# Group-norm sums taken over channels and halves of the positions on TensorE instead of over positions on VectorE

## The chip, the cores and the metric

The kernel runs on one core of one Trainium2 chip. The time is device microseconds of that core for one execution; the number that is compared is the median of several runs of the same program.

## What is computed

The input x has the shape (16, 256, 32, 32). Two layers run one after the other, each as a residual around a group norm:

```
x = x + layer0(gn(x))     # attention with 4 heads of 32, then a feed-forward part with gelu
x = x + layer1(gn(x))     # a gated state-space scan (Mamba) with 512 channels and 64 states
```

gn normalizes over 16 groups. It takes the tensor as (B, H, W, C) = (16, 256, 32, 32), so "H" is what the kernel calls its 256 channels, and a group is two neighbouring elements of the last axis:

```
g = v.reshape(B_, H_, W_, G, C_ // G)
m = mean(g, axis=(1, 2, 4));  s = var(g, axis=(1, 2, 4))
(g - m) / sqrt(s + 1e-5)
```

In the kernel an image is two tiles of 128 partitions (channels) by 1024 positions. A position p belongs to the group (p // 2) % 16. The mean of a group is thus a sum over all 256 channels and over 64 of the 1024 positions, divided by 16384. The two layers need one group norm each per image, 32 in all.

## The kernel before, in words

**The scan.** The long part is the scan of layer 1. An image is 256 units; in each, VectorE runs one scan instruction over 128 rows by 1024 positions (L928). A unit needs: a load of 512 KB from DRAM (dub, L906, seven buffers, issued six units ahead), a product on GpSimd (L911, four units ahead), a pair of bf16 matmuls into a PSUM tile of two banks (decay, L920), and the exponential of it on ScalarE (L922). There are two such PSUM tiles (pool aps), so the matmuls for unit n+2 wait until the scan of unit n has freed its tile. After each eight units the states are multiplied with C on TensorE (outputs, L953: 32 small matmuls per unit; L959 copies on ScalarE; in the first unit of the next eight, 64 small matmuls more, L965). Once per image, at units 7 and 8, ScalarE spreads C out into the tile cd that these matmuls read (spread_c, L937).

**The side stream.** While image b is scanned, everything else for image b+1 runs beside it: first_norm (the first group norm, L351 on), the gate and store of image b-1, attention_layer, and scan_inputs, which begins with the second group norm. These are Python generators. Each yield ends a step and gives its share, a length in units. The main loop turns the shares into a schedule: rate_for finds one rate so that all shares of an image fill 247 units, gap gives a step of share 1 exactly one unit, a longer one share/rate units, a shorter one its share. In each unit the order written is: load, product, outputs, scan, decay, and then the step of the side stream that is due. Each of TensorE, ScalarE, VectorE and GpSimd executes in the order in which the program was written (the last lines of the kernel chain them by hand), and the DMAs are all issued by SyncE in order.

**PSUM.** Beside the scan, psum(name) hands out one of two single banks (pool mm). Before the scan begins, the whole of image 0 is prepared with nothing beside it, and free_bank gives, in turn, a bank of mm and the two halves of a double bank of aps; a half not yet used waits in the list spare.

**The group norm** (group_norm, L259 to L297) has these steps, with their shares: sum of the first tile (1); sum of the second and the mean (1); subtract and square, once per tile (1 and 1); sum of the first square tile (1); sum of the second and the variance (1); Ln and Exp on ScalarE (2.2); multiply, once per tile (0.6 and 0.6). A sum is one reduce on VectorE over a whole tile with 16 results per partition (sum_of, L262). The sums over channels are two matmuls of the matrix avg (all 1/256) with these 16 columns (mean_of, L267). L279 scales the mean in PSUM. L281 subtracts it, L283 squares, L296 multiplies. `along` issues one DMA after each step from a list: in the first norm the loads of the position embedding and of the gate of image b-1, in the second the store of xs, the loads of rel (read by L617) and of the weights.

**Neighbours that the prediction uses.** layer_norm takes its means with pairs of 128x512 fp32 matmuls (L304) straight on the values. scan_inputs goes on after its norm with the additions of rel (L617) and the projections z (L640, two 128x512 matmuls per step). gate_and_store begins with L836 on VectorE and L840 on GpSimd.

Of the kernel before, what the change touches and what calls it, by code (L numbers as in the profile page):

```python
# [11 lines left out]
F32 = mybir.dt.float32  # L12
BF16 = mybir.dt.bfloat16
AF = mybir.ActivationFunctionType
ALU = mybir.AluOpType
AX = mybir.AxisListType
# [3 lines left out]
P = 128  # L20
C = 256
KC = C // P
L = 1024
HL = 512
NG = 16
# [25 lines left out]
def attention_then_scan_kernel(  # L51
# [18 lines left out]
    nc = tc.nc  # L70
    B = x.shape[0]

    def pool(name, bufs, **kw):
        return ctx.enter_context(tc.tile_pool(name=name, bufs=bufs, **kw))

    const = pool("const", 1)
# [4 lines left out]
    small = pool("small", 2)  # L81
# [12 lines left out]
    alone, spare = cycle((mm, aps)), []  # L94

    def bank(src, name):
        return src.tile([P, HL], F32, name=name, tag="mm" if src is mm else "av")

    def free_bank(name):
        if spare:  # L100
            return spare.pop()
        if next(alone) is mm:
            return bank(mm, name)
        both = aps.tile([P, L], F32, name=name, tag="a")
        spare.append(both[:, hs(1)])
        return both[:, hs(0)]

    def psum(name, dims=P):
        return (bank(mm, name) if beside["scan"] else free_bank(name))[:dims]
# [7 lines left out]
    def work(name, n=L):  # L117
        return wide.tile([P, L + 2 + CONV], F32, name=name, tag="wide")[:, :n]
# [4 lines left out]
    def hs(h):  # L123
        return ts(h, HL)
# [16 lines left out]
    make_identity(nc, ident)  # L141
    avg = const.tile([P, P], F32, name="avg")
    nc.vector.memset(avg, 1.0 / C)
    eps = const.tile([P, 1], F32, name="eps")
    nc.vector.memset(eps, 1e-5)

# [15 lines left out]
    for k in range(ND):  # L162
# [4 lines left out]
        for j in range(2):  # L167
# [3 lines left out]
                start=(j == 0), stop=(j == 1),  # L171
# [32 lines left out]
    t = work("ones_s")[:1]  # L204
# [3 lines left out]
    for k in range(KC):  # L208
        t = work("rel_s").rearrange("p (i j) -> p i j", j=32)
# [38 lines left out]
    def grouped(ap):  # L248
        return ap.rearrange("p (h g t) -> p h g t", g=NG, t=2)

    def over_group(s):
        return s.unsqueeze(1).unsqueeze(3).to_broadcast([P, L // (2 * NG), NG, 2])
# [4 lines left out]


    def group_norm(src, dst):  # L259
        def sum_of(part, s, k):  # L260
            view = part.rearrange("p (h g t) -> p g h t", g=NG, t=2)
            nc.vector.tensor_reduce(s[:, k, :], view, AX.XY, ALU.add)  # L262

        def mean_of(s, name):
            m = psum(f"{name}_ps")[:, :NG]
            for k in range(KC):
                nc.tensor.matmul(m, avg, s[:, k, :], start=(k == 0), stop=(k == KC - 1))  # L267
            return m

        per = C / (C * L / NG)  # L270
        s = small.tile([P, KC, NG], F32, name="gn_s", tag="gn_s")
        sum_of(src[0], s, 0)
        yield 1
        sum_of(src[1], s, 1)
        m = mean_of(s, "gn_m")
        yield 1
        s = small.tile([P, KC, NG], F32, name="gn_q", tag="gn_s")
        qs = []
        nc.vector.tensor_scalar(m, m, per, None, ALU.mult)  # L279
        for k in range(KC):  # L280
            nc.vector.tensor_tensor(grouped(dst[k]), grouped(src[k]), over_group(m), ALU.subtract)  # L281
            q = work("gn_sq")
            nc.scalar.activation(q, dst[k], AF.Square)  # L283
            qs.append(q)
            yield 1
        sum_of(qs[0], s, 0)
        yield 1
        sum_of(qs[1], s, 1)
        del qs, q
        v = mean_of(s, "gn_v")  # L290
        yield 1
        nc.scalar.activation(v, v, AF.Ln, bias=eps, scale=per)
        nc.scalar.activation(v, v, AF.Exp, scale=-0.5)
        yield 2.2
        for k in range(KC):
            nc.vector.tensor_tensor(grouped(dst[k]), grouped(dst[k]), over_group(v), ALU.mult)  # L296
            yield 0.6  # L297
# [53 lines left out]
    def first_norm(b, besides=()):  # L351
        xs, tok = [], []
        kept = state[b]["kept"] = dram.tile([C, L], F32, name="kept", tag="kept")
        if "x" in state[b]:
            xs = state[b].pop("x")
        else:
            for go in fetches(xs, x[b]):
                go()
            yield 0.4
        gn = [work("gn") for _ in range(KC)]  # L360
        yield from along(group_norm(xs, gn), fetches(tok, pos) + [None] * 3 + list(besides))
        for k in range(KC):
            nc.gpsimd.tensor_tensor(tok[k], tok[k], gn[k], ALU.add)
            nc.sync.dma_start(kept[ts(k, P), :], tok[k])
            yield 0.6
# [231 lines left out]
    def scan_inputs(b):  # L597
# [8 lines left out]
        for t in xp:  # L606
            nc.vector.memset(t[:, 0:1], 0.0)
            nc.vector.memset(t[:, L + 1 : L + 2], 0.0)
        rels = []
        yield from along(  # L610
            group_norm(xs, body),
            [partial(nc.sync.dma_start, st["xr"][ts(k, P), :], xs[k]) for k in range(KC)]
            + fetches(rels, rel) + bring,
# [274 lines left out]
    def load(n):  # L888
        b, k, q, e, i = units[n]
        st = state[b]  # L890
        if (k, q, e, i) == (0, 0, 0, 0):
            bt = hst.tile([P, L], F32, name="bt", tag="bt")
            ct = hst.tile([P, L], F32, name="ct", tag="ct")
            for v, lo in ((bt, 0), (ct, NS)):
                src = st["rows"][lo : lo + NS, :]
                nc.sync.dma_start(v, src.unsqueeze(1).to_broadcast([NS, 2, L]))
            blocks[b] = {"bt": bt, "ct": ct}
        if i == 0:
            pieces = blk.tile([P, HL], BF16, name="pieces", tag="pieces")
            rows = ds(((k * 4 + q) * 2 + e) * 48, 48)  # L900
            for hf in range(2):
                nc.sync.dma_start(pieces[ds(64 * hf, 48)], st["dps"][rows, hs(hf)])
            blocks[b, k, q, e] = pieces
        du = dutp.tile([P, L], F32, name="dub", tag="dub")
        src = st["dus"][ts(k, P)].rearrange("(q j i e) c -> q e i j c", q=4, j=2, i=SLOTS)[q, e, i]
        nc.sync.dma_start(du, src.unsqueeze(0).to_broadcast([NS, 2, L]))  # L906
        loaded[n] = du
# [87 lines left out]

    AHEAD, LEAD = 6, 4
    beside["scan"] = True
    for n in range(AHEAD):
        load(n)
    for n in range(LEAD):  # L1000
# [123 lines left out]
```

## Time and profile before

| | |
|---|---|
| median of 3 runs | 12974.16 us (12973.16 to 13009.8) |
| the profiled execution | 12999.14 us |
| its span, first to last instruction | 12997.4 us |
| first scan to last scan | 435.3 to 12948.1 us |
| VectorE busy | 11576.5 us (89%) |
| TensorE matmuls busy | 9794.6 us (75%) |
| ScalarE busy | 7531.4 us (58%) |
| GpSimd busy | 10007.5 us (77%) |
| mean granted TensorE clock | 0.799 |
| reduces of the norm (L262), 128 of them | 1.16 to 1.22 us each |

The profile is of one execution. A group in it stands for all instructions of one line and one kind, with the busy time, the mean duration, and the idle time of the engine just before them with what ended it. "PE" is the matmul part of TensorE and "PEld" its weight loads; one fp32 matmul appears as two records. The granted clock is a share of full speed. 435 us pass before the first scan; the following images take 785 to 801 us each from scan 0 to scan 0, and the last one, with little beside it, 608.

### The profile page before, as it was taken

What the parts mean: (1) busy time and instruction counts of PE and PEld (TensorE: products, weight loads), DVE (VectorE), ACT (ScalarE), POOL (GpSimd) and SP (SyncE); (2) the same over time, 40 slices, a digit from 0 to 9 for tenths busy, and PEclk for the clock granted to TensorE, in tenths of its full rate; (3) what the DMA queues carried; (4) which work ended last, traced back from release to release, by engine and by line L of the source; (5) the groups of instructions that cost most, each with busy time, mean ns of one, the idle gap of its engine ahead of it and who ended that gap; (6) DMA issues with size and microseconds to landing.
All of it is one profiled execution on the core that took longest, in us unless ns stands there. A gap on an engine that the chain in (4) does not pass through costs nothing.

```text
span 12997.4 us, 424123 instructions
## 1 busy us (share of the span) xinstructions
PE 9794.6 (75%) x186800; PEld 5486.9 (42%) x186800; DVE 11576.5 (89%) x7464; ACT 7531.4 (58%) x10421; POOL 10007.5 (77%) x4201
## 2 busy tenths in 40 slices
PE   6676877868778687786878768687786877868777
PEld 2344444444444444444444434444344444444445
DVE  3789999899999899898999999999998998989998
ACT  2465664656646566565665656656565664656654
POOL 0588877878778787787878878787787877878798
PEclk8887977878778797887879878797787978868755
DMA  1467666675666766667666666766667666676676
GB/s 51 166 218 245 206 215 224 221 243 203 212 224 220 241 204 214 230 217 239 207 228 224 217 231 211 241 210 215 225 220 241 209 215 224 224 239 202 224 252 229
DMA packets 1038400, 2820.09 MB, mean 217 GB/s; under 512 B 290370, under 2 KB 368451, under 8 KB 1036548
## 3 DMA queue, kind: packets, MB, share of 16 engines
q1 hardware_dynamic: 1036548, 2792.97, 63.2%
q8 instruction: 1459, 23.90, 0.7%
q14 instruction: 393, 3.22, 0.1%
HBM read 2513.82 MB, written 261.62 MB: 214 GB/s over the span
## 4 chain that ended last, share of the span: by engine, by line
DVE 37%; PE 29%; issue 13%; ACT 10%; DMA 7%; POOL 3%; SPq 1%; DVEq 0%; POOLq 0%; ACTq 0%
DVE h L928 26%; PE yb L953 5%; DVE mx L417 5%; ACT a L922 5%; PE a L920 4%; DMA dub<-dus 4%; PE av L492 3%; POOL dub L911 2%; PE st_ps L504 2%; PE z_ps L640 2%; PE g_ps L689 2%; PE yb L965 1%; PE m_ps L865 1%; DMA xs<-ud 1%; DVE u L675 1%
## 5 line engine op out<-in xcount | busy, mean ns | idle before, releaser
L911 POOL TENSOR_TENSOR dub<-dub,bt 128x1024 f32<-128x1024 f32 x4096 | 9781.6, 2410 | 2841.4 <-DMA dub<-dus 2555.3
L928 DVE TENSOR_TENSOR_SCAN h<-a,dub 128x1024 f32<-128x1024 f32 x4096 | 9217.0, 2280 | 798.1 <-ACT a L922 492.2
L922 ACT ACTIVATE a<-a,acol 128x1024 f32<-128x1024 f32 x4096 | 4463.0, 1090 | 3177.0 <-PE a L920 3112.4
L920 PE MATMUL a<-pieces,pick 48*128 48x512 bf16 x8192 | 1915.4, 458 | 2380.2 <-DVE h L928 2258.4
L953 PEld LDWEIGHTS yb<-h,cd 128*32 128x32 f32 x131072 | 2511.0, 129 | 2808.0 <-issue 1281.3
L953 PE MATMUL yb<-h,cd 128*32 128x64 f32 x131072 | 3283.5, 253 | 472.1 <-ACT y L959 331.8
L920 PEld LDWEIGHTS <-pick 48*128 48x128 bf16 x8192 | 606.0, 95 | 2779.1 <-issue 2368.6
L959 ACT COPY y<-yb 128x256 f32<-128x256 f32 x2048 | 763.0, 373 | 811.5 <-PE yb L953 803.5
L436 PE MATMUL s_ps<-k,q 32*64 32x512 f32 x4092 | 823.4, 617 | 93.4 <-DVE mx L417 93.4
L417 DVE TENSOR_REDUCE mx<-s_ps 128x1 f32<-128x512 f32 x1023 | 657.5, 698 | 20.0 <-PE s_ps L436 20.0
L492 PE MATMUL av<-pt,vv 128*64 128x512 f32 x2048 | 600.1, 666 | 2.8 <-ACT sums L481 1.6
L512 ACT ACTIVATE pt<-st_ps 128x512 f32<-128x512 f32 x1024 | 553.8, 597 | 71.0 <-PE st_ps L504 70.1
L965 PE MATMUL yb<-turn,y 128*32 128x16 f32 x32768 | 590.8, 214 | 4.3 <-issue 3.3
L504 PE MATMUL st_ps<-sp 33*128 33x512 f32 x2048 | 577.8, 640 | 3.3 <-ACT pt L512 3.3
L965 PEld LDWEIGHTS yb<-turn,y 128*32 128x32 f32 x32768 | 573.1, 159 | 5.1 <-issue 3.7
L969 ACT COPY yo<-yb 128x128 f32<-128x128 f32 x512 | 136.0, 266 | 627.0 <-PE yb L965 619.7
L689 PE MATMUL g_ps<-w,xp 128*128 128x256 f32 x1464 | 457.9, 452 | 0.0
L689 PEld LDWEIGHTS g_ps<-w,xp 128*128 128x128 f32 x1464 | 369.1, 326 | 67.1 <-issue 58.1
L436 PEld LDWEIGHTS s_ps<-k,q 32*64 32x64 f32 x4092 | 193.1, 130 | 435.2 <-DVE mx L417 417.0
L675 DVE SCALAR_TENSOR_TENSOR u<-up,cwh,u 128x1024 f32<-128x1024 f32 x192 | 305.1, 1589 | 27.9 <-ACT u L667 27.7
L865 PE MATMUL m_ps<-w,xs 128*128 128x256 f32 x1024 | 317.7, 460 | 11.8 <-POOL xs L840 11.8
L865 PEld LDWEIGHTS m_ps<-w,xs 128*128 128x128 f32 x1024 | 262.2, 328 | 57.6 <-issue 26.0
(177 smaller groups left out, 6805.3 us busy)
## 6 DMA issues: line engine op xcount, KB each, us to landing
dub<-dus SPq DMA_DIRECT2D x4096, 512.0 KB
dps<-pc SPq DMA_DIRECT2D x384, 128.0 KB
pieces<-dps SPq DMA_DIRECT2D x1024, 48.0 KB
xs<-in_x_dram SPq DMA_DIRECT2D x64, 512.0 KB
xs<-kept SPq DMA_DIRECT2D x64, 512.0 KB
zs<-z SPq DMA_DIRECT2D x64, 512.0 KB
ud<-u SPq DMA_DIRECT2D x64, 512.0 KB
dus<-du SPq DMA_DIRECT2D x64, 512.0 KB
```

Source lines behind the costliest of these rows:

```text
L417: nc.vector.tensor_reduce(mx[:, g, c, hf : hf + 1], s, AX.X, ALU.max)
L436: nc.tensor.matmul(waiting[g][0][ts(e, 64)], q4[r, ts(c, 64)], k4[r, hs(hf)], start=True, stop=True,)
L492: nc.tensor.matmul(av[ts(e, 2 * DH)], vv[j // (NJ // 2)][:, j % (NJ // 2), 2 * pair + e, :], pts[e], start=(j == 0), stop=(j == NJ - 1),)
L504: nc.tensor.matmul(s, ka[r, ts(j, P)], qa[r, hs(hf)], start=True, stop=True)
L689: nc.tensor.matmul(ps[:, ts(q, C)], xp[k][:, ds(first + t, P, 4)], wg_s[:, k, t, :], start=(k == 0 and t == 0), stop=False,)
L911: nc.gpsimd.tensor_tensor(v, v, blocks[units[n][0]]["bt"], ALU.mult)
L920: nc.tensor.matmul(a[:, hs(hf)], w, pieces[r], start=True, stop=True)
L922: nc.scalar.activation(a, a, AF.Exp, scale=acol[:, at : at + 1])
L928: nc.vector.tensor_tensor_scan(now["h", e][:, i, :], decays.pop(n), loaded.pop(n), 0.0, ALU.mult, ALU.add)
L953: nc.tensor.matmul(yb[ts(g, 32), ts(s, 64)], cd[:, at // 16, ts(c, 32)], hbuf[:, :, at : at + 8], start=(c == 0), stop=(c == 1),)
L959: nc.scalar.copy(y2[:, r], yb[:, :256])
L965: nc.tensor.matmul(some[ts(r, 32), x], y2[:, r, x:256:8], turn[:, x], start=True, stop=True)
```

## The change

The sums of the norm are no longer taken over positions first. sum_of now gives the values themselves, 512 columns at a time, to TensorE as the moving operand, against a new constant matrix share (all 1/16384): for each of the two tiles and each half of the positions, one 128x512 matmul, all four added up in one PSUM bank. This leaves 512 column sums, the same on all partitions. mean_of then reduces these 512 to 16 on VectorE (one reduce from PSUM into a small SBUF tile). For the mean, ScalarE copies the 16 numbers back into the first columns of the bank, where L281 reads them as before; the scaling L279 is gone, since share has the whole factor. For the variance, Ln reads the 16 numbers from SBUF and writes PSUM. The mean gets a step of its own (share 1), and the reduce for the variance moves into the step of Ln and Exp. The bank of each norm half is taken at the first sum instead of after the second. spare is emptied when the scan begins.

```
+    share = const.tile([P, P], F32, name="share")
+    nc.vector.memset(share, 1.0 / (C * L / NG))
...
     def group_norm(src, dst):
-        def sum_of(part, s, k):
-            view = part.rearrange("p (h g t) -> p g h t", g=NG, t=2)
-            nc.vector.tensor_reduce(s[:, k, :], view, AX.XY, ALU.add)
-
-        def mean_of(s, name):
-            m = psum(f"{name}_ps")[:, :NG]
-            for k in range(KC):
-                nc.tensor.matmul(m, avg, s[:, k, :], start=(k == 0), stop=(k == KC - 1))
+        def sum_of(part, sums, k):
+            for h in range(2):
+                nc.tensor.matmul(
+                    sums, share, part[:, hs(h)],
+                    start=(k == 0 and h == 0), stop=(k == KC - 1 and h == 1),
+                )
+
+        def mean_of(sums):
+            m = small.tile([P, NG], F32, name="gn_s", tag="gn_s")
+            nc.vector.tensor_reduce(
+                m, sums.rearrange("p (h g t) -> p g h t", g=NG, t=2), AX.XY, ALU.add
+            )
             return m

-        per = C / (C * L / NG)
-        s = small.tile([P, KC, NG], F32, name="gn_s", tag="gn_s")
+        s = psum("gn_m_ps")
         sum_of(src[0], s, 0)
         yield 1
         sum_of(src[1], s, 1)
-        m = mean_of(s, "gn_m")
-        yield 1
-        s = small.tile([P, KC, NG], F32, name="gn_q", tag="gn_s")
+        yield 1
+        m = s[:, :NG]
+        nc.scalar.copy(m, mean_of(s))
+        yield 1
         qs = []
-        nc.vector.tensor_scalar(m, m, per, None, ALU.mult)
         for k in range(KC):
             nc.vector.tensor_tensor(grouped(dst[k]), grouped(src[k]), over_group(m), ALU.subtract)
             q = work("gn_sq")
             nc.scalar.activation(q, dst[k], AF.Square)
             qs.append(q)
             yield 1
+        s = psum("gn_v_ps")
         sum_of(qs[0], s, 0)
         yield 1
         sum_of(qs[1], s, 1)
         del qs, q
-        v = mean_of(s, "gn_v")
-        yield 1
-        nc.scalar.activation(v, v, AF.Ln, bias=eps, scale=per)
+        yield 1
+        v = s[:, :NG]
+        nc.scalar.activation(v, mean_of(s), AF.Ln, bias=eps)
         nc.scalar.activation(v, v, AF.Exp, scale=-0.5)
         yield 2.2
...
     AHEAD, LEAD = 6, 4
     beside["scan"] = True
+    spare.clear()
```

## The prediction

> **What bounds the kernel now.** I read the page first, then the two tiles of the group norm, then the windows of the norms, and last the timeline unit by unit. From the page, the engine totals and the costliest groups (after the bar: busy time, mean ns of one, idle time before it and who ended it):
>
> ```profile
> PE 9794.6 (75%) x186800; PEld 5486.9 (42%) x186800; DVE 11576.5 (89%) x7464; ACT 7531.4 (58%) x10421; POOL 10007.5 (77%) x4201
> ...
> L928 DVE TENSOR_TENSOR_SCAN h<-a,dub 128x1024 f32<-128x1024 f32 x4096 | 9217.0, 2280 | 798.1 <-ACT a L922 492.2
> L922 ACT ACTIVATE a<-a,acol 128x1024 f32<-128x1024 f32 x4096 | 4463.0, 1090 | 3177.0 <-PE a L920 3112.4
> L920 PE MATMUL a<-pieces,pick 48*128 48x512 bf16 x8192 | 1915.4, 458 | 2380.2 <-DVE h L928 2258.4
> ```
>
> VectorE is the busiest, and three engines form a ring: a decay matmul (L920) waits for a scan (L928) two units back to free its PSUM tile, ACT waits for that matmul, and a later scan waits for ACT. From the starts of the scans: a unit with nothing beside it lasts 2.20 us, one with a reduce of the norm (L262) 3.31, one with L279 and L281 3.53, one with L281 alone 3.31. So in the norms VectorE work is paid in full: 1.11 us for a reduce, 0.22 for L279. The view of the tile gn_s gives durations (ns, min/median/max):
>
> ```profile
> L267 PE MATMUL gn_m_ps<-gn_s,avg x128: 262/376/396, 21.2 to 12042.9; 128*128 128x16 f32 x128
> L262 DVE TENSOR_REDUCE gn_s<-xs x64: 1162/1208/1221, 20.0 to 12041.4; 128x16 f32<-128x1024 f32 x64
> ```
>
> An fp32 matmul leaves two matmul records (x128 for 32 norms of two matmuls). The windows of one first norm and one second norm (PE, PEld, DVE, ACT, POOL busy; then TensorE's granted clock):
>
> ```profile
> 1224.70:1240.40 15.70, 8.71 (x144) 5.65 (x143) 15.67 (x13) 7.24 (x9) 15.70 (x8) 0.50 0.92 314
> ...
> 1707.60:1725.50 17.90, 9.58 (x178) 6.32 (x177) 17.87 (x18) 8.64 (x11) 10.72 (x5) 0.55 0.88 298
> ```
>
> VectorE is full, and TensorE is at half clock in almost all of the norm. What two 128x512 fp32 matmuls cost at that clock is in the timeline just after this norm (start, duration):
>
> ```profile
> 1724.34 1.20 DVE L262 TENSOR_REDUCE gn_q<-gn_sq 128x16 f32<-128x1024 f32 x1
> ...
> 1748.35 0.61 PE L920 MATMUL a<-pieces,pick 48*128 48x512 bf16 x2 [7.54 <-DVE h L928]
> ...
> 1748.89 3.78 PE L640 MATMUL z_ps<-xp,w 128*128 128x512 f32 x4
> ...
> 1752.60 1.08 PE L953 MATMUL yb<-h,cd 128*32 128x64 f32 x32
> ...
> 1753.34 0.69 DVE L630 SCALAR_TENSOR_TENSOR z<-z_t,z_ps 128x512 f32<-128x512 f32 x1 [0.68 <-ACT z_t L645]
> 1753.61 0.11 PEld L920 LDWEIGHTS <-pick 48*128 48x128 bf16 x2 [0.17 <-issue]
> 1753.61 0.49 PE L920 MATMUL a<-pieces,pick 48*128 48x512 bf16 x2
> ...
> 1754.04 1.99 PE L640 MATMUL z_ps<-xp,w 128*128 128x512 f32 x4
> 1754.15 1.09 ACT L922 ACTIVATE a<-a,acol 128x1024 f32<-128x1024 f32 x1 [0.85 <-PE a L920]
> ...
> 1755.34 2.29 DVE L928 TENSOR_TENSOR_SCAN h<-a,dub 128x1024 f32<-128x1024 f32 x1 [1.32 <-ACT a L922]
> ```
>
> The first pair takes 3.78 us, holds up the next decay matmul by 4.7, and the scan behind that waits. The second pair, 5.3 us or more after TensorE began, takes 1.99.
>
> [...] Decay matmuls of 0.39 us turn into 0.58 to 0.61 about two units after the last large matmul. [...] The nearest row, the maxima of L417 (128x512 from PSUM), has 0.70. I take 0.66[...].
>
> **The change part by part.** There are 32 norms. Two are in the part before the scan; 30 run beside it, in 15 images a first norm (units 1 on) and a second one (units 160 on).
>
> Removed: four reduces (4 x 1.11) and L279 (0.22), so 4.66 us of VectorE per norm beside the scan, 140 us in 30. Four small matmuls (8 records) go too; behind the reduces they cost nothing.
>
> Added: per norm eight 128x512 matmuls (16 records), a pair to a step; two reduces of 0.66; a ScalarE copy of 128x16 (0.17 as L293 to 0.25 as L292), which comes while the scan before L281 runs. One step more per norm: 228 shares become 230, and the rate of the schedule goes from 1.164 to 1.183. An image still has 256 units, so this only closes two empty ones. It moves Ln and Exp one unit later.
>
> A half (mean or variance) at full clock, T the end of the scan in whose unit the first pair is issued: decay T+0.1, pair 0.3 later to T+2.4, output matmuls, decay at T+2.9 (2.5 after the pair's start, as in the L640 units 1756.86 to 1759.36), second pair T+3.2 to 5.2, reduce to T+5.95, scan. Without side work that scan starts at T+4.4: cost 1.55.
>
> A half at half clock first: pair T+0.6 to 4.4, next decay T+5.3, second pair T+5.75 to 7.75 at full clock, reduce to T+8.5, scan. Cost 4.1. The reduce stands one unit after the second pair, too near to be free.
>
> Second norm. Its first unit is warm (L920 0.39 us in 14 of 15 images), so the mean half costs 1.55 against 2.44 (two reduces, L279): gain 0.9. Two subtractions later, some 10 us, TensorE is cold, so the variance half costs 4.1 against 2.22: loss 1.9. Behind it Ln and Exp (3.0 us with two table loads) now stand right before the unit with the 64 turning matmuls (168), whose output copy queues behind them on ScalarE and holds the decay matmul; that adds up to 2.4. On the other side the L617 pair (3.3 us each beside busy POOL, 1.22 alone) is now split over units 170 and 171 and finds POOL nearer to done, and the first pair of L640, which today stalls the scan anyway, absorbs more: its scan moves from 1755.34 to about 1756. I take +1 (bounds -1 and +3.6).
>
> First norm. Both mean steps fall into unit 1 (the trace has both reduces there), and TensorE is cold: eight records, about 5.5 at 0.86 and the rest at 0.43, some 6.0 us. With the scan end at 1224.74: records 1225.35 to 1231.4, reduce to 1232.1, scan 3 at 1232.15. It starts today at 1230.43, with L279 and one subtraction (1.33) already done: loss 2.8 on equal work. The variance half is cold again: loss 1.9. So scan 8 goes from 1244.73 to 1249.5. Then Ln falls between the two spreading copies of L937 (2 x 1.36) and the first of them also waits for the second pair; the outputs of unit 8 wait for both, the decay matmul for them: scan 11 moves from 1257.08 to about 1264. I take +6.5 (bounds +2.8, no tail and a quicker clock, and +8).
>
> Beside the scan: 15 x (6.5 + 1) = 112. Before the scan nothing covers the norms: for the first, the second input lands at 25.6; a cold pair 3.8, reduce 0.66, copy 0.3 give the subtraction at 30.5, today 27.75 (L281); two pairs and the reduce after the squares put Ln at 39.2, today 33.15. That is +6; the second I take at +5. Total 112 + 11 = 123; for waits on gate loads and POOL that take up some of it I subtract 8: **+115**.
>
> DMAs: in the second norm rel and the weights keep their units, in the first the gate loads are issued a unit earlier against their use. DMA is 0.9 busy there, the same bytes, so I count nothing. The new constant costs one memset (0.17 us as L143) before the scan. spare.clear() removes nothing: 193 banks are asked for before the scan in both kernels, given in threes, and 193 leaves no half over.
>
> The profiled execution took 12999.14 us for a span of 12997.4; the median of the runs is 12974.16, 0.2% less. The sum is a difference and applies to either: 12974 + 115 = 13089, say **13090**.
>
> **The rivals.**
> (a) The clock stays full through the norms[...]. Against it: it is cold two units after the last long matmul. Then three of the four halves of an image's two norms cost 1.55: gains of 0.9, 0.7 and 0.7. In the fourth, the first norm's mean, eight records of 0.43 end 3.5 us after 1225.05, scan 3 starts at 1229.55, a loss of 0.3 on equal work. That is 2.0 x 15 = 30 us of gain, less 8 before the scan: **12952**. It decides where the first variance pair lasts about 2 us instead of 3.8. Chance 0.08.
> (b) VectorE's time is all that counts, and the matmuls hide in TensorE's gaps (1.7 us idle ahead of L920 in a unit of 3.31): a reduce of 0.66 costs 0.6, so 4.66 - 2 x 0.6 = 3.46 per norm, 104 us in 30, less 11 before the scan: **12881**, faster than before. Against it: the pair stands between one decay matmul and the next, in the ring, and the reduce comes one unit later. It decides where both halves of a norm together make VectorE wait less than 3.46 us. Chance 0.07.
> (c) The loss is half absorbed: later waits (L836 on DMA 124 us in all, POOL on dub) shrink[...]: +15 to +60, **13012**. Chance 0.12.
> (d) TensorE stays cold in the second pairs too (3.78 instead of 1.98 in about 45 halves, 1.8 each, 81 us more): **13170**. Chance 0.05.
> The forecast itself: 0.68.
>
> **How the numbers follow.** The main case spans 13020 to 13135: the first norm between +4 and +8, the second between -1 and +2.5, 15 times, and +3 outside. 12990 to 13165 adds most of (c) and half of (d), and leaves out (a), (b) and the rest: 0.2. About 0.3% (39 us) is what a measurement of this kernel can tell from no change. Faster: (b) and a quarter of (a), 0.09. Same: the rest of (a), half of (c), a little of the main case, 0.13. Slower: 0.78.
>
> **What would show it.** Right: sum matmuls of some 0.9 us a record in units 1 and 165, of 0.43 in 160; VectorE idle before the reduce of the sums, released by PE, 2 to 3 us each time in a variance half; scans 3 to 11 of an image later against its scan 0 by up to 7 us; VectorE busy down by about 32 x (4 x 1.2 + 0.17 - 2 x 0.66) = 117 us while the span grows. Wrong: a clock near 1 in the windows of the norms, reduces that wait for nothing, or first norms no longer than 15.7 us from the first sum to the last.

## The result and the profile after

The changed kernel takes 12932.41 us (median of 15 runs, 12900.57 to 12992.08) against 12976.08 before (15 runs). The ratio is 0.9966, with a 95% interval of 0.9955 to 0.9978: 44 us faster, where 115 us slower were forecast. The profiled execution took 12932.41 us for a span of 12930.6.

Behind the norm the line numbers are 6 higher than before: the scan is L934, its exponential L928, the decay matmul L926, the product of GpSimd L917, the additions of rel L623, the sums of the norm L264, the reduce L271. The profile counts matmul records, two to an fp32 matmul: the 32 and 64 small matmuls of a unit named above are 16 and 32 in the program. The page of the changed kernel, engine totals and the groups that answer to those shown of before:

```profile
PE 9895.0 (77%) x187056; PEld 5464.7 (42%) x187056; DVE 11351.6 (88%) x7369; ACT 7519.9 (58%) x10453; POOL 10023.3 (78%) x4201
...
L934 DVE TENSOR_TENSOR_SCAN h<-a,dub 128x1024 f32<-128x1024 f32 x4096 | 9195.8, 2274 | 739.5 <-ACT a L928 411.1
L928 ACT ACTIVATE a<-a,acol 128x1024 f32<-128x1024 f32 x4096 | 4463.9, 1090 | 3068.5 <-PE a L926 3027.9
L926 PE MATMUL a<-pieces,pick 48*128 48x512 bf16 x8192 | 1877.0, 449 | 2283.2 <-DVE h L934 2170.7
```

The ring is as it was. VectorE is busy 225 us less; the forecast said 117. From the waits of VectorE (us in total, times, longest) and the timeline of the first norm beside image 1's scan and of a later second norm (start, duration; in brackets what the engine waited for):

```profile
DVE gn_s L271 <- PE gn_m_ps L264: 98.8, 33, 9.9
DVE gn_s L271 <- PE gn_v_ps L264: 96.5, 31, 5.4
```

```profile
1234.65 6.23 PE L264 MATMUL gn_m_ps<-xs,share 128*128 128x512 f32 x8
...
1240.91 0.69 DVE L271 TENSOR_REDUCE gn_s<-gn_m_ps 128x16 f32<-128x512 f32 x1 [4.55 <-PE gn_m_ps L264]
...
1251.02 3.78 PE L264 MATMUL gn_v_ps<-gn_sq,share 128*128 128x512 f32 x4
...
1256.28 2.24 PE L264 MATMUL gn_v_ps<-gn_sq,share 128*128 128x512 f32 x4
...
1258.56 0.69 DVE L271 TENSOR_REDUCE gn_s<-gn_v_ps 128x16 f32<-128x512 f32 x1 [3.77 <-PE gn_v_ps L264]
...
4873.08 1.98 PE L264 MATMUL gn_m_ps<-xs,share 128*128 128x512 f32 x4
...
4875.90 1.99 PE L264 MATMUL gn_m_ps<-xs,share 128*128 128x512 f32 x4
4877.92 0.69 DVE L271 TENSOR_REDUCE gn_s<-gn_m_ps 128x16 f32<-128x512 f32 x1 [0.80 <-PE gn_m_ps L264]
...
4888.03 3.78 PE L264 MATMUL gn_v_ps<-gn_sq,share 128*128 128x512 f32 x4
```

Inside the norms this is much what the forecast described: eight records in the first norm's mean that begin at half clock (granted 0.50 from 1234.65 to 1239.0, then 0.85 from 1239.3 to 1240.9; 6.23 us in all, forecast 6.0), a warm mean in the second norm (granted 1.00; 1.98 and 1.99, and much the same in 13 of the 15 images), cold first pairs in the variances (granted 0.50 in both that are shown; 3.25 to 3.78 beside the scan), VectorE waiting mostly 2.3 to 4.8 us for the cold halves. So the norms seem to cost time, and the gain must come from somewhere else. The busy time of VectorE, compared line by line, shows where to look. The reduces and L279 give 115 us (the forecast's 117). The other 110 us are in instructions that the change doesn't touch, chiefly the additions of rel and the taps of the convolution (87 us of it). First the kernel before, then after, from the groups of VectorE:

```profile
L675 DVE SCALAR_TENSOR_TENSOR u<-up,cwh,u 128x1024 f32<-128x1024 f32 x192 | 305.1, 1589 | 27.9 <-ACT u L667 27.7
...
L617 DVE TENSOR_TENSOR xp<-xp,xs 128x1024 f32<-128x1024 f32 x32 | 88.6, 2809 | 0.0
```

```profile
L681 DVE SCALAR_TENSOR_TENSOR u<-up,cwh,u 128x1024 f32<-128x1024 f32 x192 | 261.7, 1363 | 28.0 <-ACT u L673 27.7
```

The views of the line of the rel additions, before and after, have minimum, median and maximum in ns:

```profile
L617 DVE TENSOR_TENSOR xp<-xp,xs x32: 1221/3338/3362, 293.1 to 12071.7; 128x1024 f32<-128x1024 f32 x32
...
L623 DVE TENSOR_TENSOR xp<-xp,xs x32: 1193/1200/3380, 308.0 to 12013.6; 128x1024 f32<-128x1024 f32 x32
```

The median was 3.34 us before and is 1.20 now. Nothing in these instructions changed, only what runs beside them. Both additions stood in unit 170 of an image and stand in units 170 and 171 now. Of an image's twelve taps and the four instructions that close them (L718), six stand one unit later and ten in the same unit as before.

### The profile page after: what moved, and what is told of

Its sections match the earlier page's. It is cut to its first block, busy times and chain, and to the rows that moved or that the text cites. A ratio compares the mean times of both kernels' runs of the same rounds, so it can differ in the third digit from the quotient of the medians.

```text
span 12930.6 us, 424775 instructions
## 1 busy us (share of the span) xinstructions
PE 9895.0 (77%) x187056; PEld 5464.7 (42%) x187056; DVE 11351.6 (88%) x7369; ACT 7519.9 (58%) x10453; POOL 10023.3 (78%) x4201
## 4 chain that ended last, share of the span: by engine, by line
DVE 35%; PE 32%; issue 12%; ACT 10%; DMA 6%; POOL 3%; SPq 1%; DVEq 0%; POOLq 0%; ACTq 0%
DVE h L934 25%; PE yb L959 6%; DVE mx L423 5%; PE a L926 5%; ACT a L928 5%; DMA dub<-dus 3%; PE g_ps L695 3%; PE av L498 3%; POOL dub L917 2%; PE st_ps L510 2%; PE m_ps L871 2%; PE z_ps L646 2%; DMA xs<-ud 1%; PE yb L971 1%; PE gn_v_ps L264 1%
## 5 line engine op out<-in xcount | busy, mean ns | idle before, releaser
L917 POOL TENSOR_TENSOR dub<-dub,bt 128x1024 f32<-128x1024 f32 x4096 | 9797.6, 2415 | 2716.7 <-DMA dub<-dus 2415.0
L934 DVE TENSOR_TENSOR_SCAN h<-a,dub 128x1024 f32<-128x1024 f32 x4096 | 9195.8, 2274 | 739.5 <-ACT a L928 411.1
L928 ACT ACTIVATE a<-a,acol 128x1024 f32<-128x1024 f32 x4096 | 4463.9, 1090 | 3068.5 <-PE a L926 3027.9
L926 PE MATMUL a<-pieces,pick 48*128 48x512 bf16 x8192 | 1877.0, 449 | 2283.2 <-DVE h L934 2170.7
L959 PEld LDWEIGHTS yb<-h,cd 128*32 128x32 f32 x131072 | 2432.7, 126 | 2804.6 <-issue 1313.7
L959 PE MATMUL yb<-h,cd 128*32 128x64 f32 x131072 | 3186.7, 248 | 447.6 <-ACT y L965 282.1
L926 PEld LDWEIGHTS <-pick 48*128 48x128 bf16 x8192 | 601.8, 95 | 2670.4 <-issue 2290.7
L681 DVE SCALAR_TENSOR_TENSOR u<-up,cwh,u 128x1024 f32<-128x1024 f32 x192 | 261.7, 1363 | 28.0 <-ACT u L673 27.7
```

The costliest lines, as they stand in the source:

```text
L917: nc.gpsimd.tensor_tensor(v, v, blocks[units[n][0]]["bt"], ALU.mult)
L926: nc.tensor.matmul(a[:, hs(hf)], w, pieces[r], start=True, stop=True)
L928: nc.scalar.activation(a, a, AF.Exp, scale=acol[:, at : at + 1])
L934: nc.vector.tensor_tensor_scan(now["h", e][:, i, :], decays.pop(n), loaded.pop(n), 0.0, ALU.mult, ALU.add)
L959: nc.tensor.matmul(yb[ts(g, 32), ts(s, 64)], cd[:, at // 16, ts(c, 32)], hbuf[:, :, at : at + 8], start=(c == 0), stop=(c == 1),)
```

## The experiments

All comparisons are ratios to the kernel before on the same chip; a ratio is turned into microseconds with 12976. Its interval is 0.09 to 0.23% each way, 12 to 30 us, and a difference between two kernels, taken from two such ratios, is less certain than either. Times per image are means over images 1 to 14, from the starts of the scans in two profiled executions. In the expectations, P is the forecast's mechanism (the sums are paid for as worked out), S that the extra step moves later steps to other units, and Q that what these moved steps meet there is GpSimd's product; other letters are explained where they stand.

### The step without the sums: step_only

The kernel before, with one empty step behind the mean of each norm, so that every later step falls into the unit that it has in the changed kernel.

```
         m = mean_of(s, "gn_m")
         yield 1
+        yield 1
```

> The kernel before with one empty step of share 1 in each norm, where the change has its extra step; no other part of the change. Theory P: within 20 us of before, rel and taps within 10% of before. Rival S: faster by 60 us or more, with rel near 45 and taps near 262 us busy.

Measured: 12877.35 us, ratio 0.9924 (0.9911 to 0.9936), 99 us faster than before. S holds and P falls as an account of the result. This kernel computes exactly what before did, in the same instructions: an extra step that does nothing is worth more than the whole change. Against it the changed kernel is 55 us slower (0.9966 against 0.9924). Per image, changed against step_only, scan 3 of an image is 2.86 us later against its scan 0, scan 8 is 4.30 later, scan 11 is 4.59 later; in the second norm, counted from scan 156, scan 164 is 0.86 earlier and scan 168 0.70 later.

### Each norm alone: n1_only, n2_only, and their controls step1, step2

The change in the first or the second norm only, the other with its reduces. First the call sites of the change in the first norm alone (group_norm_old is the former function); the second kernel exchanges the two.

```
-            group_norm(xs, body),
+            group_norm_old(xs, body),
```

> The change in the first norm of an image only; the second norm as before. Theory P (the matmuls and the reduce that waits for them cost what was forecast in the norms, and the time came back later, behind the second norm, where two-input VectorE instructions waited less for GpSimd because the second norm leaves GpSimd a shorter lead): slower than before by 60 to 95 us (5.6 us in each of 15 images up to unit 11, some 8 before the scan), and the additions of rel (90 us busy in 32 before) and the taps (305 us in 192) stay within 10% of before. Rival T (the delay in the first norm is what shifts GpSimd against VectorE): taps and rel drop as in the changed kernel, to some 262 and 45 us, time -20 to -60 us. Rival S (the extra step in the schedule does it): half of the drop, time about 0.

> The change in the second norm of an image only; the first norm as before. Theory P: faster than before by 90 to 140 us: the sections after unit 168 lose what they lose in the changed kernel (9 to 10 us an image), the first norm's +5.6 is absent; rel and taps at some 45 and 262 us busy. Rival T: rel and taps as before, time +10 to +30 us. Rival S: about half of the drop.

Measured: 13068.67 us, ratio 1.008 (1.0063 to 1.0096), and 13030.44 us, 1.0044 (1.0031 to 1.0056). Each half of the change alone makes the kernel slower (104 and 57 us), both together make it faster by 44. That can't be a sum of two costs. P's expectations missed: for the first kernel the time is a little above its range, and the additions of rel, which were to stay within 10% of 90 us, take 74; the second was to be 90 to 140 us faster. No rival had either time. The controls have the empty step in one norm only:

```
-    def group_norm(src, dst):
+    def group_norm(src, dst, pause=False):
...
+        if pause:
+            yield 1
```

> The kernel before with one empty step (share 1) after the mean, in the first norm only: the control for the change in the first norm alone (13068.67 us), with the same steps in the same places. Theory P (on an equal schedule the new sums cost what the prediction said, a little less): the first norm on TensorE costs 4.6 us per image in 15 images and 8 to 15 us before the scan, so this kernel stands 75 to 90 us below 13069, at 12980 to 12995. Rival: the empty step alone does nothing in the first norm that isn't there with the whole change; the 93 us of the change in the first norm are all its own, and this kernel is at 12975 within 10 us all the same. What separates: a time below 12950 or above 13010 would say that the step of one norm moves other steps into better or worse units by itself.

> The kernel before with one empty step in the second norm only: the control for the change in the second norm alone (13030.44 us). Theory P: on an equal schedule the second norm on TensorE costs -1 to +1 us per image and 5 to 8 us before the scan, so this kernel lies 0 to 25 us below 13030, at 13005 to 13030, which would be slower than before by the schedule alone. Rival: the schedule does nothing with one norm's step, this kernel is at 12975, and the change in the second norm costs 55 us of its own, 3 us per image.

Measured: 13014.1 us, 1.002 (1.0009 to 1.0031), and 12994.32 us, 1.0008 (0.9997 to 1.002). The step of one norm alone gives no gain at all. In these two kernels and in n1_only and n2_only both additions of rel still stand in unit 170, in 14 of 14 images, and all 32 together take 71 to 76 us, against 90 before and 47 in step_only. On equal steps the first norm costs 0.60% or 78 us (expected 75 to 90), with scan 11 of an image 4.80 us later; the absolute time of step1 was outside what was expected for it. The second costs 0.36% or 47 us, more than the 0 to 25 expected, although the trace has it no dearer than with both: the stretch from scan 160 to 168 is 0.76 longer and the next, to 172, 0.94 shorter. P was wrong on its size here; the ledger below puts the 47 us elsewhere.

### Only the two additions moved: rel_apart

Both additions of rel stood in unit 170. With a whole step between them they stand in two units; nothing else of the kernel before is edited.

```
-            yield 0.6
+            yield 1
```

> The kernel before with the two additions of rel (L617) one unit apart (share 1 instead of 0.6 each); nothing else. Theory Q (an instruction of VectorE with two SBUF inputs waits for a GpSimd product that is running, and the schedule decides how often; the extra step moved the two additions into two units, with a scan between them): rel falls from 90 us busy to below 60, time -25 to -75 us. Rival (the gain of the empty step comes from elsewhere, such as the taps or waits on DMA): rel stays above 80 us and the time within 20 us.

Measured: 12951.85 us, ratio 0.9982 (0.9973 to 0.9991). The view of the line in this kernel:

```profile
L617 DVE TENSOR_TENSOR xp<-xp,xs x32: 1194/1234/2186, 279.8 to 12030.9; 128x1024 f32<-128x1024 f32 x32
```

The additions are quick again, and the stretch from scan 168 to 172 is 3.18 us shorter per image, exactly as in step_only. But only 23 us come out in all (25 to 75 were expected), since the stretch from 130 to 160 is now 5.06 longer. The waits of VectorE name that: the softmax denominators go to DRAM and back twice (few, sums). Before, then rel_apart:

```profile
DVE few L536 <- DMA few<-den: 116.7, 12, 109.1
...
DVE ao L548 <- DMA sums<-den: 22.8, 16, 6.3
```

```profile
DVE few L536 <- DMA few<-den: 142.2, 16, 98.6
...
DVE ao L548 <- DMA sums<-den: 60.9, 16, 5.7
```

Without the longest wait of few, in the part before the scan, the round trips cost 30 us before and 104 us here. In before, in step_only and in the changed kernel the load of few is issued in unit 136 and its reciprocal stands in unit 137; in rel_apart, step1, step2, step_three, n1_only, n2_only and late_reduce both stand in one unit, in 14 of 14 images, and of the second trip the last load and the first use stand one unit apart instead of two. The steps between them have shares of a half, and whether two of these share a unit depends on the fraction of a unit at which the first one falls.

### The cause of the slow additions: noprod_before, noprod_step, noprod_after

These three are before, step_only and the changed kernel without GpSimd's product dub x bt, in every unit but the first (what they compute is therefore another).

```
-        nc.gpsimd.tensor_tensor(v, v, blocks[units[n][0]]["bt"], ALU.mult)
+        if n < 1:
+            nc.gpsimd.tensor_tensor(v, v, blocks[units[n][0]]["bt"], ALU.mult)
```

> The kernel before without the product on GpSimd (L911 is left out for all units but the first, so the scan runs on the loaded values and the output is another). Theory Q: rel is 1.2 us each time (39 us in 32), the taps 1.25 (240 us in 192), and the time falls by 100 us or more. Rival (they are slow for another reason, their operands or DMA): rel stays near 2.8 us each.

> The same without the product, with the empty step of share 1 in each norm. Theory Q: no contention is left for the schedule to change, so within 30 us of the kernel without the product and without the step (96 us apart with the product). Rival (the schedule's gain lies in waits on DMA or TensorE): 60 us or more faster than that kernel.

> The changed kernel without the product on GpSimd. Theory P (matmuls and the waiting reduce cost what the trace says on an equal schedule: 4.6 us in each first norm, 0 to 0.7 in each second, 15 before the scan): slower by 60 to 100 us than the kernel with the empty step and without the product. Rival: the matmuls cost nothing once GpSimd is out of the way: within 20 us of it.

Measured: 12678.71, 12661.49 and 12735.06 us (ratios 0.9773, 0.9757, 0.9810, each within about 0.0023). Without the product the empty step is worth 17 us by the medians, not 99, and the two intervals overlap, so that it may be nothing; Q holds. The changed kernel then costs 74 us over its control, within P's range; its fastest run is 43 us above the slowest of the control. Views of the lines in noprod_before:

```profile
L617 DVE TENSOR_TENSOR xp<-xp,xs x32: 1198/1217/1220, 281.9 to 11767.6; 128x1024 f32<-128x1024 f32 x32
...
L675 DVE SCALAR_TENSOR_TENSOR u<-up,cwh,u x192: 1251/1259/1285, 308.0 to 11867.2; 128x1024 f32<-128x1024 f32 x192
```

No addition and no tap is slow where the product is absent. The timelines show the meeting itself, instruction by instruction; the kernel before in image 1, then step_only in the same place:

```profile
1739.37 2.37 POOL L911 TENSOR_TENSOR dub<-dub,bt 128x1024 f32<-128x1024 f32 x1
1739.47 3.34 DVE L617 TENSOR_TENSOR xp<-xp,xs 128x1024 f32<-128x1024 f32 x1
...
1741.68 3.33 POOL L911 TENSOR_TENSOR dub<-dub,bt 128x1024 f32<-128x1024 f32 x1
...
1742.74 3.36 DVE L617 TENSOR_TENSOR xp<-xp,xs 128x1024 f32<-128x1024 f32 x1
...
1744.98 3.32 POOL L911 TENSOR_TENSOR dub<-dub,bt 128x1024 f32<-128x1024 f32 x1
```

```profile
1734.28 2.33 POOL L912 TENSOR_TENSOR dub<-dub,bt 128x1024 f32<-128x1024 f32 x1
1735.90 1.79 DVE L618 TENSOR_TENSOR xp<-xp,xs 128x1024 f32<-128x1024 f32 x1
...
1736.57 3.32 POOL L912 TENSOR_TENSOR dub<-dub,bt 128x1024 f32<-128x1024 f32 x1
...
1739.82 1.19 DVE L618 TENSOR_TENSOR xp<-xp,xs 128x1024 f32<-128x1024 f32 x1
...
1739.85 3.36 POOL L912 TENSOR_TENSOR dub<-dub,bt 128x1024 f32<-128x1024 f32 x1
```

In one unit the two additions alternate with the products: each addition ends about 1.1 us after the product that was running when it began, and each product behind them lasts 3.3 us instead of 2.35. Apart, the first addition meets only the last 0.7 us of a product (1.79 us), and the second begins just ahead of the next product: it keeps its 1.19 us, and the product is the one that lasts longer (3.36).

### The reduce one unit later: late_reduce and its control step_three

The changed kernel with a step more ahead of each of its two reduces, so that VectorE need not wait for TensorE; and before with three empty steps in the same places.

```
         sum_of(src[1], s, 1)
         yield 1
+        yield 1
...
         del qs, q
         yield 1
+        yield 1
```

> The changed kernel with one more empty step ahead of each reduce of the sums, so that TensorE is done when VectorE comes to it. Theory P: the idle time of VectorE before that reduce (195 us in the changed kernel, 64 times) falls below 70 us, and the time below the changed kernel's by 30 to 90 us, that is -70 to -140 us against before. Rival R (the wait only moves: the decay matmuls behind the pairs hold the scan anyway, because TensorE is the one that is late): the idle time before the reduce goes, that before the scan for ScalarE grows by as much, and the time stays within 20 us of the changed kernel's.

> The kernel before with three empty steps per norm (two after the mean, one before Ln): the steps of the changed kernel with its two reduces one unit later (13094.48 us), without its sums on TensorE. Theory P: if the sums cost the same 40 to 60 us as with one step, with two halves whose reduce no longer waits 3 us, this kernel is 20 to 60 us below, at 13035 to 13075, and slower than before by the schedule alone. Rival: the schedule of three steps is as good as that of one (12877 to 12975), and the later reduces themselves cost 120 us or more.

Measured: 13094.48 us, ratio 1.0092 (1.0078 to 1.0106), and 12995.33 us, 1.0004 (0.9991 to 1.0018). The waits ahead of the reduce did fall, from 98.8 and 96.5 us to 45.9 and 5.4. Yet the time is 1.26% above the changed kernel's, where P expected a time 30 to 90 us below that kernel's and rival R one within 20 us of it. On equal steps the sums cost 0.88%, 114 us: the expectation of 20 to 60 was wrong, and step_three's time came nearer to the rival's. Per image, scan 11 is 3.91 later than in the control, little less than without the later reduce, and the stretch from scan 160 to 168 is 3.73 longer. A likely reason, which no run tests: the matmuls still stand in the ring ahead of the decay matmul, and a reduce that finds them done doesn't take them out of it. Why the second norm lost 3 us by it stays open.

### The one warm half alone: warm_mean

step_only, with the sums on TensorE for the mean of the second norm beside the scan and nowhere else.

```
+        if warm and beside["scan"]:
+            m = psum("gn_m_ps")
+            for k in range(KC):
+                for h in range(2):
+                    nc.tensor.matmul(
+                        m, share, src[k][:, hs(h)],
+                        start=(k == 0 and h == 0), stop=(k == KC - 1 and h == 1),
+                    )
+                yield 1
```

> The kernel before with one empty step per norm, and with the sums on TensorE only for the mean of the second norm beside the scan, the one half of the four per image that finds TensorE's clock full. Theory P: 0.6 to 0.9 us less per image, 10 to 13 us in all, against the kernel with the empty step alone (12877.35 us): 12864 to 12868, below both kernels. Rival: what the shorter half gains is given back at the next wait (the first subtraction or the projections), and the time is 12877 within 5 us.

Measured: 12863.5 us, ratio 0.9902 (0.9883 to 0.9922), the fastest of the kernels that have the product. The view of the tile of the sum (ns, minimum/median/maximum):

```profile
L277 PE MATMUL gn_m_ps<-xs,share x120: 592/592/1220, 904.6 to 11909.7; 128*128 128x512 f32 x120
```

Counted from scan 156, scan 168 of an image comes 0.87 us earlier than in step_only, as worked out (0.9). Part of it is given back elsewhere: the stretch from scan 0 to 156 is 1.27 us longer, for a reason that stays open, and a whole image 0.63 shorter. That its time is below step_only's isn't shown by the runs alone, since the two intervals overlap; both beat the changed kernel.

### A ledger

For each kernel against before: the time of four kinds of VectorE instruction that read two SBUF operands (rel, L675, L718, L836; 628.4 us before, 439 to 440 us in all three kernels without the product; two more kinds, L548 and L572, stay within 4 us of their 78 us before in every kernel with the product), the waits for the round trips (30.4 us before), and what remains of the measured difference. It counts both terms as paid in full, which is an assumption, and it sets one profiled execution beside a median, so the last column is good to some 20 us at best. It is roughest for n1_only, whose profiled execution took 53 us more than its median and began its first scan at 465.6 us, against 436.1 in step1.

| kernel | measured, us | two-operand work | round trips | rest |
|---|---|---|---|---|
| step_only | -99 | -96 | +6 | -8 |
| changed | -44 | -121 | +4 | +72 |
| step1 | +26 | -48 | +83 | -8 |
| n1_only | +104 | -54 | +75 | +83 |
| step2 | +10 | -60 | +76 | -6 |
| n2_only | +57 | -2 | +70 | -11 |
| rel_apart | -23 | -75 | +74 | -22 |
| step_three | +5 | -15 | +77 | -56 |
| late_reduce | +119 | -4 | +76 | +47 |
| warm_mean | -127 | -110 | +10 | -27 |

The rest is the cost of the new sums plus whatever the step does by itself. Against its control it is +80 for the changed kernel, +91 for the first norm, -5 for the second, +103 for the late reduces, -19 for the warm half; without the product +74 was measured directly. By this account the second norm's 47 us were not its sums: with them the two-operand work met GpSimd more often again (58 us more than in step2). In step_three some 4.65 us per image were won in the first eleven units by a cause that stays open.

## Why the prediction was wrong

**The step that failed** is the sentence on the added step: "An image still has 256 units, so this only closes two empty ones." It was costed at nothing, without a name for the work that hides it. The two steps shift what follows, and that was worth -99 us in step_only, of the opposite sign to the forecast's sum: instructions that the forecast had not listed met GpSimd's product less often (by the ledger 96 us of the 99; without the product the same steps gave 17 by the medians). A step in one norm alone gave no gain. The forecast had the piece in hand: it wrote that the L617 pair takes "3.3 us each beside busy POOL, 1.22 alone" and is now split over two units. But it let this vanish in a +1 for the second norm. Two additions back at 1.2 us are 4.2 us per image by its own figures; the trace shows 3.2 to 3.9 between scans 168 and 172. It didn't ask which other instructions spread as widely (before, the taps from 1.25 to 3.46 us, L718 from 1.20 to 3.43, L836 from 1.26 to 2.71), nor treat the schedule as an unknown with two ends.

**The clock and the waits** were right in the main. On equal steps scan 3 is 2.86 us later (forecast 2.8), scan 8 4.30 (4.7); the second norm's mean wins 0.86 (0.9), its variance loses 1.55 (1.9). The 0.66 us for a reduce of 512 values from PSUM was the author's estimate; in before, the maxima of L417 took 0.67 to 0.74, and the new reduces (L271) took 0.69. Rival (a) decides at a first variance pair of 2 us; it lasts 3.25 to 3.78. Rival (d) fell too: second pairs of the variances take 1.98 to 2.24 beside the scan. Rival (b) needed VectorE to wait less than 3.46 us per norm; it waited 6.1.

**The terms that were mis-sized.** The tail of the first norm, where Ln falls between the copies of spread_c, was to bring scan 11 to +6.5; it is 4.59 to 4.80, so 0.3 us instead of 1.8 came after scan 8. The first norm was thus taken too dear by about 27 us over 15 images. The second norm, +1 with its tail, is about nothing at scan 172 (+0.70 at 168, then -0.71). The part before the scan, +11, cost about 15 (first scan at 450.2 us against 435.4 in step_only and 435.3 before; but executions of kernels with the old norm there have it anywhere from 422 to 437, and n1_only, with one new norm there, has it at 465.6, so this term is rough). The 8 us taken off for absorption were not identified. On equal steps the change costs 55 us as measured and about 74 to 80 once the two-operand work is set apart, where 115 were forecast.

**The rivals** (b) and (a) gave a faster kernel for reasons that did not happen; the measured 12932 lies near (a) by number only. No rival had the schedule as its mechanism.

**What would show it** spoke mostly in favour of the forecast, except that the span did not grow and that VectorE was busy 225 us less instead of 117. That surplus of 110 us, in lines outside the diff, was the sign.

## What to carry to other kernels

In a kernel whose side work is laid out over fixed units, an added step is a change to every later step: cost it as an unknown of its own, by listing the instructions whose durations spread widely and the round trips whose ends stand near each other, and compare the edit with a control that has its steps but not its work. Here that control was faster than the change it was made for. The same durations also say what to try on purpose: keep VectorE instructions like these, with two SBUF operands, away from GpSimd's products (an addition of 1.20 to 1.22 us without them took up to 3.38 beside them), and keep a unit between a load and its use (the round trips cost 30 us in before and 104 in rel_apart).

## What the runs showed of the hardware

The additions of rel and the taps, VectorE instructions with two SBUF operands, and GpSimd's products last longer where they meet. A 128x1024 fp32 addition takes 1.20 to 1.22 us without the product (noprod_before) and up to 3.38 beside a product (which takes 2.35 us by itself and 3.3 behind an addition), a tap 1.26 and up to 3.46, and with the product gone all 192 taps lie between 1.251 and 1.285. The trace of step_only shows both orders. Where an addition or a tap began with more than 0.3 us of a product to go (43 times), it ended 1.08 to 1.09 us after that product; where a product began with more than 0.3 us of an addition or a tap to go (183 times), it ended 2.20 to 2.26 us after it, so the one that began second lasted longer. Two kinds that read a PSUM tile and an SBUF tile lasted no longer beside the product. Of the 4096 scans of before, 2789 began with more than 0.3 us of a product to go; they took 2.28 us on average, as did all of them (2275 ns in noprod_before). Of the 64 subtractions of the means (L281, 128x1024), 44 began so, and all 64 took 1.20 to 1.22. No run shows by what means the two engines hold each other up.

What had not been expected is that the number of such meetings changes so much with so little. Additions and taps that began with more than 0.3 us of a product to go were 77 in before, 43 in step_only and 27 in the changed kernel. The sum of the four kinds ran from 508 to 628 us over the kernels with the product, and the DMA round trips of the same bytes cost 30 us in before, where the first load and its use stood in neighbouring units, and 104 in rel_apart, where they stood in one.
